# Residual rows of a graph layer: their stores and loads emitted two or three steps later

## The chip, the core and the metric

The kernel runs on one core of a Trainium2 chip. A core has five engines with a queue of instructions each: TensorE (PE) for matrix products, VectorE (DVE), ScalarE (ACT), GpSimd (POOL) and SyncE (SP). They wait for each other only through semaphores. Transfers between the main memory and the core's on-chip memory are issued from the queues of SyncE, ScalarE and GpSimd and carried out by 16 DMA engines. TensorE writes to eight banks of accumulators.

The metric is the device time of one execution in microseconds. A profile shows one execution, instruction by instruction; a time is the median of several executions.

## What is computed

The input `x` holds 8 graphs' features for 4096 nodes and 256 features, `adj` is one matrix of 4096 x 4096, mostly zeros, and `W` is 256 x 256.

```python
HW = jnp.einsum('bnf,fo->bno', x, W)
A_norm = relu((adj + adj.T) * 0.5)
D = jnp.sum(A_norm, axis=1)
d = where(D > 0, D ** -0.5, 0)
L_norm = eye(N) - d[:, None] * A_norm * d[None, :]
out = relu(jnp.einsum('nm,bmo->bno', L_norm, HW))
return layernorm(x + out, axis=-1)      # over the 256 features
```

## The kernel before

**Two stages.** The first symmetrises the matrix block by block, writes it to main memory (`a_dram`), forms the products of features and weights, scaled by the node's degree, and writes them there too (`g_dram`, 4096 rows of 2048 numbers: 8 graphs times 256 features). It also works out, from the pattern of zeros, which rows each block of outputs needs.

The second stage, from about 583 us on, works through the output in 32 blocks of 128 nodes. Block 0 is done in the first stage. The others go in **units** of two blocks, `2u+1` (b0) and `2u+2` (b1), in the order of `SEQ`; the last unit has one block. A unit is a list of **steps**. Each step multiplies gathered rows: a *full* step is four products over the whole array for one block, from a gathered tile or from one of two tiles kept on the chip (hubs); a *row-tiled* step packs up to eight small products of 64 rows x 32 columns, each for four accumulator banks. A gathered tile is 128 rows of `g_dram` (1 MB), fetched by two indirect transfers on GpSimd's queue (lines 956 and 964) into a ring of 12 buffers; a buffer is asked for again once its tile is used up.

**After the products of a block**, `finish` empties its four banks through ScalarE into `y` (line 772, one buffer). VectorE then adds the block's residual row tile `xr` (line 782; 128 nodes x 8 graphs x 256 features, 1 MB), computes mean and variance (line 791) and normalises in place (line 815). SyncE stores the result (line 825). The `xr` tile was loaded before by `residual` (line 766) from ScalarE's queue, into a pool of four buffers which rotates, so that a unit's loads take the buffers of the unit two before it. The last block (31) has its row loaded by GpSimd and is finished by a function of its own.

**What is emitted when.** The program is written out step by step in the loop at line 1209. `after(n, ...)` puts a call on a list; `run_later(2)`, called after each step, lowers each entry by 2 and makes the calls that have 2 or less left. At the start of a unit three calls are put there: `prepare` (6), which gives VectorE the work on the lists of later units, and two of `exchange`. One `exchange` stores the oldest finished block of the unit before (if there is one) and loads the rows that it is given: the first call those of b0, the second those of b1. `finish` itself puts `rest`, the VectorE part of a block, two further on, and `lists` goes there when a unit's b0 is complete: TensorE then counts and places rows for later units (line 430) from what VectorE prepared.

**Order within a queue.** `with queue("act")` and its like pin an instruction behind the last one emitted for that engine. A row-tiled step ends each of its four rounds with a tick, a no-op on ScalarE (line 1206) that waits for TensorE's products of the round; two rounds later TensorE's products wait for it (`follow`). A full step puts nothing into ScalarE's queue. So whatever is emitted for ScalarE after a step stands behind the ticks of the last row-tiled step and behind the last emptying of banks.

**Steps of the units**, in running order, F for full and T for row-tiled, the first seven steps of each: unit 1 and unit 7 FTFFTFT; units 2, 3, 4 and 6 FTFFFTF; unit 5 FTFTFTF; unit 8 FTFTFTT; units 9 to 14 FTFFFTT. Unit 0 and the last unit, 15, load no rows by this path. These units have 11 to 28 steps (unit 15 has 4); b0 ends one or two steps before b1.

Of the kernel before, what the change touches and what calls it, by code (L numbers as in the profile page):

```python
# [67 lines left out]
def kernel(  # L68
# [49 lines left out]
    def blocks(u):  # L118

        return min(2, NB - 1 - 2 * u)  # L120
# [777 lines left out]
    with (  # L898
# [38 lines left out]
        def load_hub_rows(units, h, b):  # L937

            u = next((v for v in units if HUBS[v] > h), None)
            if u is None:  # L940
                return
            i = 2 * u + 1 + b
            with queue("pool"):
                nc.gpsimd.dma_start(
                    hub_rows[h][b], a_dram[h * P : (h + 1) * P, i * P : (i + 1) * P]
                )
            got[u, -1 - h, b] = (hub_rows[h][b], hubs[h], 0, False)
# [26 lines left out]
        def gather_ahead():  # L974
            nonlocal asked, eaten
            while eaten < asked and not uses_left[order[eaten]]:
                eaten += 1
            while asked < len(order) and asked - eaten < RING:
                gather(asked)
                asked += 1  # L980
            if asked == len(order) and asked - eaten < RING and NB - 1 not in xr:
                xr[NB - 1] = ring[asked % RING].rearrange("p (b f) -> p b f", b=B)
                with queue("pool"):
                    nc.gpsimd.dma_start(
                        xr[NB - 1], x[:, (NB - 1) * P :, :].rearrange("b p f -> p b f")
                    )
# [4 lines left out]
        def after(n, fn, *args):  # L991
            later.append((n, fn, args))

        def run_later(by):
            ready = [l for l in later if l[0] <= by]
            later[:] = [(n - by, fn, args) for n, fn, args in later if n > by]
            for _, fn, args in ready:
                fn(*args)
# [63 lines left out]
        def finish(i):  # L1062

            if i == NB - 1:
                while later:
                    run_later(1)
                while finished:
                    exchange([])
                finish_last(i)
                return  # L1070
            with queue("act"):
                y = evict(i, py.pop(i), ypool)

            def rest():
                z = xr.pop(i)
                with queue("dve"):
                    mv, var = moments(i, y, z, stat)
                with queue("dve"):
                    rstd = inverse_root(i, var, stat)

                in_turn(normalise, i, z, mv, rstd)
                finished.append((i, z))

            after(2, rest)
# [80 lines left out]
        def product(u, op, c, ps, cols, start, stop):  # L1165

            t, _, b, _ = op
            at, gt, apart, one = got[u, t] if t >= 0 else got[u, t, b]
            off = -cols.start if one else b * apart
            with queue("pe"):  # L1170
                return nc.tensor.matmul(  # L1171
                    py[2 * u + 1 + b][c][cols, :],
                    lhsT=at[ps, off + cols.start : off + cols.stop],
                    rhs=gt[ps, c * S : (c + 1) * S],
                    start=start,
                    stop=stop,
                    skip_group_check=True,
                )
# [4 lines left out]
        def tiled(u, step, last):  # L1183

            for m in range(NC):
                ins = None
                for i in range(2):
                    c = (m + 2 * i) % NC
                    for op in step:
                        if op[1] != i:  # L1190
                            continue
                        before = ins
                        ins = product(
                            u,
                            op,
                            c,
                            slice(i * L, (i + 1) * L),
                            slice(op[3] * E, (op[3] + 1) * E),
                            False,
                            op in last and m >= NC // 2,  # L1200
                        )
                        if before is None:
                            if len(ticks) > 1:
                                follow(ins, ticks[-2])
                with queue("act"):
                    ticks.append(nc.scalar.nop())
                follow(ticks[-1], ins)

        for q, (u, step) in enumerate(steps):
            new = q == 0 or steps[q - 1][0] != u  # L1210
            if new:
                after(6, prepare, u)
                rows = [2 * u + 1 + b for b in range(2)] if q > 0 and blocks(u) == 2 else []
                if q == 0:
                    after(8, exchange, [])
                elif rows:
                    after(6, exchange, rows[:1])
                    after(10, exchange, rows[1:])
                else:
                    after(2, exchange, [])  # L1220
                    after(4, exchange, [])
                left, begun = {}, set()
                for v, st in steps[q:]:
                    if v == u:
                        for _, _, b, j in st:
                            for e in range(QU) if j is None else [j]:
                                left[b, e] = left.get((b, e), 0) + 1
                for b in range(blocks(u)):
                    py[2 * u + 1 + b] = []
            touched = sorted({b for _, _, b, _ in step})  # L1230
            for b in touched:
                if not py[2 * u + 1 + b]:
                    py[2 * u + 1 + b] = [
                        psum.tile([P, S], F32, tag=f"b{b}", name=f"py_{u}_{b}_{c}") for c in range(NC)
                    ]
            if step[0][1] is None:
                (op,) = step
                b = op[2]
                hs = {(b, e) for e in range(QU)}
                assert not hs & begun or hs <= begun  # L1240
                for h in hs:
                    left[h] -= 1
                for c in range(NC):
                    product(
                        u, op, c, slice(0, P), slice(0, P), not hs & begun, not any(left[h] for h in hs)
                    )
                begun |= hs
            else:
                for op in step:
                    assert op[2:] in begun  # L1250
                    left[op[2:]] -= 1
                last = [op for op in step if not left[op[2:]]]
                tiled(u, step, last)
            for op in step:
                t = op[0]
                uses_left[u, t] -= 1
                if t < 0:
                    load_hub_rows(SEQ[SEQ.index(u) + 1 :], -1 - t, op[2])
            gather_ahead()
            run_later(2)  # L1260
            for b in touched:
                if not any(left[b, e] for e in range(QU)):
                    if b == 0:
                        after(2, lists, u)
                    finish(2 * u + 1 + b)
# [67 lines left out]
```

## Time and profile before

| | us |
|---|---|
| median of 3 timed runs | 1755.12 |
| lowest, highest | 1754.09, 1763.07 |
| the profiled execution's own time | 1499.77 |
| its span, first to last instruction | 1497.7 |
| TensorE busy in it | 1386.5 |
| VectorE busy | 1041.9 |
| GpSimd busy | 766.3 |
| ScalarE busy | 361.2 |
| 28 residual loads from ScalarE, first and last issue | 677.0, 1422.5 |
| 31 stores from SyncE, first and last issue | 595.7, 1474.9 |

The profiled execution took 255 us less than the median of the timed runs; its mean granted clock of TensorE was 0.971. The DMA engines moved 543.04 MB at a mean of 363 GB/s.

In the profile's lines a name such as `xr<-in_x_dram` reads "written from", `L766` is a line of the kernel, and `[5.33 <-...]` is the idle time of the engine ahead of the instruction and what ended it. ACTq and SPq are the queues of ScalarE and SyncE, where transfers are issued. Forty slices of equal length show each engine's busy share in tenths.

### The profile page before, as it was taken

The page shows a single profiled execution, that of the slowest core. Times are in us where ns is not written, and L with a number is a line of the kernel's source. Part 1 is how long each engine was busy: PE and PEld are TensorE (multiplying, and loading weights), DVE is VectorE, ACT ScalarE, POOL GpSimd, SP SyncE. Part 2 cuts the span into 40 slices and gives each one's busy share as a digit, 9 for nine tenths or more (in the row PEclk, how much of TensorE's full clock was granted, in tenths as well). Part 3 has the DMA queues.
Part 4 walks back from the last instruction along what each step waited for, and adds up shares of the span by engine and source line. Part 5 has one row for each costly group of instructions (what it writes and reads, how often), then busy time and mean ns, then how long its engine had stood idle before and what let it go on. Part 6 is the DMA issues. An engine that isn't in the chain of part 4 may idle for free.

```text
span 1497.7 us, 29688 instructions
## 1 busy us (share of the span) xinstructions
PE 1386.5 (93%) x11008; PEld 746.5 (50%) x11008; DVE 1041.9 (70%) x3173; ACT 361.2 (24%) x462; POOL 766.3 (51%) x1564
## 2 busy tenths in 40 slices
PE   7999979999999989999999999999998999898993
PEld 6777857876777753443433333333333333333331
DVE  4677578779594863119477888789229989979554
ACT  4555544554444450010101100100010011011111
POOL 2435010011222326765775777777556776777662
PEclk9999999999999999999999999999999999998996
DMA  9999999998998999999999999999879999999993
GB/s 349 364 377 381 402 402 352 379 379 322 385 370 323 338 381 361 387 390 345 368 384 343 385 401 375 375 391 385 354 262 345 341 373 406 383 351 396 384 378 136
DMA packets 217159, 543.04 MB, mean 363 GB/s; under 512 B 19369, under 2 KB 109193, under 8 KB 182425
## 3 DMA queue, kind: packets, MB, share of 16 engines
q0 software_dynamic: 55664, 283.87, 49.2%
q1 hardware_dynamic: 93472, 126.89, 24.6%
q10 hardware_dynamic: 67872, 130.32, 23.1%
q8 instruction: 89, 1.46, 0.4%
q14 instruction: 62, 0.51, 0.1%
HBM read 438.03 MB, written 136.34 MB: 383 GB/s over the span
## 4 chain that ended last, share of the span: by engine, by line
PE 58%; DMA 21%; DVE 13%; issue 3%; ACT 2%; POOL 2%; ACTq 0%; DVEq 0%; POOLq 0%
PE py L1171 34%; PE pg L606 10%; DMA g<-g_dram,gi 9%; PE lead L564 6%; DMA a_dram<-sym 5%; PE tr L495 3%; PE xtr L595 3%; DVE sym L499 3%; DMA xr<-in_x_dram 3%; DMA xin<-in_x_dram 2%; DVE sums L506 1%; DVE stats L791 1%; DMA ga<-a_dram,ai 1%; DVE xr L782 1%; ACT sym L503 1%
## 5 line engine op out<-in xcount | busy, mean ns | idle before, releaser
L1171 PE MATMUL py<-g,ga 64*32 64x512 f32 (+1 forms) x7136 | 623.3, 610 | 32.0 <-DMA g<-g_dram,gi 28.9
L1171 PEld LDWEIGHTS py<-g,ga 64*32 64x32 f32 (+1 forms) x7136 | 226.3, 114 | 412.6 <-issue 335.9
L956 POOL DMA_INDIRECT ga<-a_dram,ai x268 | 295.4, 1102 | 139.5 <-PE py L1171 67.6
L964 POOL DMA_INDIRECT g<-g_dram,gi x268 | 292.3, 1091 | 117.9 <-issue 71.3
L772 ACT ACTIVATE y<-py,minus_r 128x512 f32<-128x512 f32 x120 | 72.8, 689 | 793.3 <-PE py L1171 551.8
L606 PE MATMUL pg<-w_sb,xt 128*128 128x256 f32 x1024 | 231.2, 384 | 9.3 <-ACT xt L596 9.3
L1171 PE MATMUL py<-g_hub,gh 128*128 128x512 f32 x480 | 220.7, 601 | 5.3 <-DVE pos_k L239 5.3
L606 PEld LDWEIGHTS pg<-w_sb,xt 128*128 128x128 f32 x1024 | 195.2, 193 | 36.7 <-ACT xt L596 10.2
L499 DVE TENSOR_TENSOR sym<-tr,adj 128x512 f32<-128x512 f32 x256 | 162.9, 683 | 66.3 <-PE tr L495 53.8
L506 DVE TENSOR_REDUCE sums<-sym 128x64 f32<-128x2048 f32 x64 | 145.5, 2280 | 58.7 <-ACT sym L503 58.7
L507 POOL TENSOR_SCALAR uses<-sums 128x64 uint8<-128x64 f32 x64 | 24.4, 381 | 268.5 <-DVE sums L506 222.5
L1171 PEld LDWEIGHTS py<-g_hub,gh 128*128 128x128 f32 x480 | 87.6, 190 | 133.0 <-issue 119.7
L495 PE MATMUL tr<-ident,adj 128*128 128x128 f32 x1024 | 136.4, 281 | 17.1 <-DVE sym L499 10.9
L503 ACT ACTIVATE sym<-sym 128x2048 f32<-128x2048 f32 x64 | 122.5, 1915 | 110.4 <-DVE sym L499 104.4
L442 DVE TENSOR_SCALAR low<-lists 128x17 f32<-128x17 f32 (+8 forms) x14 | 2.5, 176 | 202.4 <-PE lists L430 202.4
L495 PEld LDWEIGHTS tr<-ident,adj 128*128 128x128 f32 x1024 | 115.7, 143 | 48.2 <-DVE sym L499 28.7
L782 DVE TENSOR_TENSOR xr<-xr,y 128x2048 f32<-128x2048 f32 x31 | 70.9, 2287 | 51.9 <-ACT y L772 39.3
L595 PE MATMUL xtr<-ident,xin 128*128 128x128 f32 x512 | 73.7, 291 | 19.4 <-DVE sym L499 11.9
L815 DVE TENSOR_SCALAR xr<-xr,mv,root 128x256 f32<-128x256 f32 x248 | 85.2, 416 | 1.1
L791 DVE BATCH_NORM_STATS2 stats<-xr 128x6 f32<-128x256 f32 x248 | 84.1, 412 | 1.1
L564 PE MATMUL lead<-gt,strip 128*128 128x512 f32 x176 | 83.3, 593 | 0.0
L596 ACT COPY xt<-xtr 128x512 f32<-128x512 f32 x128 | 68.1, 592 | 61.3 <-PE xtr L595 59.9
(157 smaller groups left out, 1057.9 us busy)
## 6 DMA issues: line engine op xcount, KB each, us to landing
adj<-in_adj_dram SPq DMA_DIRECT2D x64, 1024.0 KB, 12.2
a_dram<-sym ACTq DMA_DIRECT2D x64, 1024.0 KB, 8.8
out_dram<-xr SPq DMA_DIRECT2D x31, 1024.0 KB, 22.9
xr<-in_x_dram ACTq DMA_DIRECT2D x28, 1024.0 KB, 13.2
xin<-in_x_dram SPq DMA_DIRECT2D x44, 512.0 KB, 11.2
g_dram<-gt ACTq DMA_DIRECT2D x22, 1024.0 KB, 8.0
xin<-in_x_dram POOLq DMA_DIRECT2D x20, 512.0 KB
g_dram<-held ACTq DMA_DIRECT2D x10, 1024.0 KB, 10.2
```

What stands on the lines that cost most here:

```text
L495: ins = nc.tensor.transpose(pt[:, c * P : (c + 1) * P], tji[:, c, a * P : (a + 1) * P], ident)
L499: nc.vector.tensor_add(sym[:, a, :], pt, tij[:, a, :])
L503: nc.scalar.activation(sym, sym, AF.Relu, scale=0.5)
L506: nc.vector.tensor_reduce(sums, sym.rearrange("p a (c q) -> p a c q", q=E), AX.X, ALU.add)
L564: nc.tensor.matmul(lead[c], lhsT=strip, rhs=g[:, c * S : (c + 1) * S], start=not done, stop=len(done) == NB - 1, skip_group_check=True,)
L595: nc.tensor.transpose(pt[:, k, c, :], xin[b // H][:, b % H + k, c * P : (c + 1) * P], ident)
L606: ins = nc.tensor.matmul(pg[:, k * FO : (k + 1) * FO], lhsT=xt[:, b + k, c, :], rhs=w_sb[:, c, :], start=(c == 0), stop=(c == FC - 1),)
L782: nc.vector.tensor_add(z, z, y)
L791: nc.vector.bn_stats(stats[:, b, :], z[:, b, :])
L956: nc.gpsimd.indirect_dma_start(out=at if both else at[:, : E if one else P], out_offset=None, in_=a_pairs if both else a_groups if one els ...
L964: nc.gpsimd.indirect_dma_start(out=gt, out_offset=None, in_=g_dram, in_offset=bass.IndirectOffsetOnAxis(ap=gi[:, t : t + 1], axis=0), boun ...
L1171: return nc.tensor.matmul(py[2 * u + 1 + b][c][cols, :], lhsT=at[ps, off + cols.start : off + cols.stop], rhs=gt[ps, c * S : (c + 1) * S], ...
```

## The change

Two numbers in the loop at line 1209. For units 1 to 14 the two calls of `exchange` are put on the list at 8 and 14 instead of 6 and 10, so that they are made after the steps 3 and 6 of a unit, counted from 0, instead of 2 and 4. The calls for unit 0 and for the last unit stay.

```diff
                 if q == 0:
                     after(8, exchange, [])
                 elif rows:
-                    after(6, exchange, rows[:1])
-                    after(10, exchange, rows[1:])
+                    after(8, exchange, rows[:1])
+                    after(14, exchange, rows[1:])
                 else:
                     after(2, exchange, [])
                     after(4, exchange, [])
```

## The prediction

> **What bounds the kernel now.** I read the page first (slices, waits), then the timelines of ScalarE, SyncE and VectorE around the moved transfers, the waits of TensorE step by step, the DMA share of one unit, and last the chain of waits near the end. Units are counted in running order, 0 to 15, steps within a unit from 0.
>
> ```profile
> span 1497.7 us, 29688 instructions
> ...
> PE   7999979999999989999999999999998999898993
> ...
> DVE  4677578779594863119477888789229989979554
> ...
> DMA  9999999998998999999999999999879999999993
> ```
>
> The changed stage begins at 583 us (slice 16). TensorE is the bound in it, at nearly full share, with the DMA engines full beside it and VectorE near full in slices 30 to 36. So a moved transfer matters only where TensorE waits for data or where VectorE is late. ScalarE's timeline shows where the residual loads (line 766) really go out:
>
> ```profile
> 1131.24 0.37 ACTq L766 DMA_DIRECT2D xr<-in_x_dram  x1
> ...
> 1173.58 1.01 ACTq L766 DMA_DIRECT2D xr<-in_x_dram  x2
> ...
> 1225.98 1.09 ACTq L766 DMA_DIRECT2D xr<-in_x_dram  x2
> ```
>
> In units 9 and 10 (second and third line) both loads of a unit leave 0.4 us apart, though they are emitted two steps apart. A load enters ScalarE's queue behind the last tick (the no-op of line 1206), and only a row-tiled step has ticks; a full step of four products has none. Ten of the fourteen units that load begin full, tiled, full, full, full, so both loads hang on the tick of step 1.
>
> The stores are different. VectorE's and SyncE's timelines:
>
> ```profile
> 1186.75 2.02 DVE L815 TENSOR_SCALAR xr<-xr,mv,root 128x256 f32<-128x256 f32 x6
> ```
> ```profile
> 1188.79 0.37 SPq L825 DMA_DIRECT2D out_dram<-xr  x1
> ```
>
> The normalisation ends at 1188.77 and the store goes at 1188.79. SyncE has nothing else to do, so all 31 stores follow their data within 0.1 us, wherever they are emitted.
>
> TensorE's waits of this stage, here in step 8 of unit 9, and the DMA around it:
>
> ```profile
> 1197.21 1.05 PE L1171 MATMUL py<-g,ga 64*32 64x512 f32 x4 [0.25 <-ACTq L1206]
> 1201.64 4.73 PE L1171 MATMUL py<-g,ga 64*32 64x512 f32 x54 [3.38 <-DMA g<-g_dram,gi]
> ```
> ```profile
> 1180.00:1193.00 13.00, 11.90 (x113) 3.95 (x111) 12.18 (x69) 0.00 (x0) 8.96 (x11) 1.00 1.04 407
> 1193.00:1206.00 13.00, 9.08 (x122) 3.16 (x128) 12.52 (x32) 0.00 (x0) 9.67 (x9) 0.87 1.04 397
> ```
>
> The last three columns are granted clock, DMA share and GB/s: TensorE waits for a gather exactly where the DMA is full, and afterwards runs at a lower clock. A step lasts 3.4 us; this one takes 8.7.
>
> The chain of waits near the end names the other side, a load that is late, and VectorE's timeline shows what its add waited:
>
> ```profile
> 1377.28 0.38 ACTq L766
> 1377.75 45.14 DMA xr<-in_x_dram
> 1423.02 2.30 DVE xr L782
> ```
> ```profile
> 1423.02 2.29 DVE L782 TENSOR_TENSOR xr<-xr,y 128x2048 f32<-128x2048 f32 x1 [5.33 <-DMA xr<-in_x_dram]
> ```
>
> So the second load of unit 13 takes 45 us and is already late. The page's 13.2 us to landing is a median over the few loads it could pair, mostly first ones.
>
> **What the Trainium skill says.** "DMA: Bandwidth & Descriptors", section Queues, rings and completion order: each DMA engine takes turns between the queues that have work, and one queue's descriptors are consumed in ring order. The trace agrees: of the two loads issued at 1173.6 and 1174.0, the packets that close the first have landed by 1185.9 and those of the second by 1205.6. The same page, Issuing engines are not separate DMA queues: loads, stores and gathers share the 16 engines, as the 1.04 share shows. "TensorE: Matmul & The Clock Gate", HAM oscillation: a wait of some microseconds on data drops the clock to half for a while; the clock records here have half-clock windows of 3.4 to 6.8 us at 942, 997, 1201 and 1297, each at a wait for a gather.
>
> **The change, part by part.** Nothing is added or removed. The list is drained by 2 after each step: a due value of 6 fires after step 2, 10 after step 4, 8 after step 3, 14 after step 6.
>
> 1. Stores: emitted later, issued when the data is there; the normalisations end before or near the new place and SyncE has no other work. Cost 0.
>
> 2. First loads: from behind the last tick up to step 2 to the last tick up to step 3. This differs only where step 3 is tiled, in units 5 and 8: from 912.9 to 920.1 and from 1124.1 to 1131.2. Elsewhere 0.
>
> 3. Second loads, the real change. From the last tick up to step 4 to the last one up to step 6. Taking the end of that step in the trace of before plus 1.1 us (tick), unit by unit, issue before, issue after, and landing of the first load of the pair (from the ScalarE queue's packets):
> unit 1: 687.8, 694.8, 682.6; unit 2: 742.5, 756, 748.3; unit 3: 805.6, 819, 812.3; unit 4: 859.6, 873, 879.0; unit 5: 920.1, 927.3, 931.5; unit 6: 969.4, 983, 984.8; unit 7: 1031.8, 1038.9, 1039.5; unit 8: 1131.2, 1141.8, 1129.4; unit 9: 1174.0, 1193.2, 1185.9; unit 10: 1226.4, 1243.4, 1249.8; unit 11: 1273.9, 1293.1, 1288.8; unit 12: 1328.7, 1345.6, 1343.7; unit 13: 1377.8, 1394.7, 1398.4; unit 14: 1422.5, 1434.1, 1437.3.
> So the second load is issued up to 19 us later, but where the first is still in flight then (units 4, 5, 6, 7, 10, 13, 14) it stood in line behind it anyway, and moves nothing. It really starts later by 7 to 13 us in units 1, 2, 3 and 8, 7.3 in 9, 4.3 in 11, 1.9 in 12.
>
> Lateness: before, the second load landed ahead of its add by 40 to 52 us (units 1 to 3), 33 (8), 24.4 (9), 9.4 (10), 20.1 (11), 7.1 (12), 0.7 (13), 0.6 (14). All real shifts fit. Cost 0; if cover is gone, see the second rival.
>
> Gathers: in unit 9 the queue of the loads moves 0.37 MB in 1186 to 1193, which is put behind the gathers that step 8 waits for. At 400 GB/s that is 0.9 us. Unit 11 likewise, 4.3 us at about 60 GB/s, 0.26 MB, 0.6 us. Unit 8: by its wait near 1150 both loads were through; after, about 0.3 MB of the second is not, 0.8 us. Unit 5: the first load starts 7 us later, 0.3 MB, 0.8 us. Sum -3.1 us. Bounds: no more than a whole load, 1.05 MB, can be put behind a wait, 2.6 us in each of units 5 to 11, so -18; and on the other side, early in units 8 and 9 the DMA has spare room (share 0.65 at 1120 to 1125, 0.78 at 1170 to 1175) that the later load no longer uses and asks back where it is full, at most those same two loads, +5.
>
> ScalarE's queue: the issue now stands between the ticks of steps 6 and 7. It takes 0.37 us (0.99 at most) and a semaphore wait of 0.02 before it, and TensorE asks for a tick only two product groups, 0.8 us each, later. 0. The wait for a free buffer held unit 14's second load from 1416.7 to 1422.5 before; its new time is past that. No gain, nothing was waiting there. POOL's queue is untouched; it holds no moved instruction.
>
> Sum: 1497.7 + 2.1 around the span = 1499.8 for the profiled execution, less 3.1, 1496.7. The median of the timed runs is 1755.1, 255 us above; the profile does not say why. I carry the sum over by the ratio 1.17: -3.6 us, 1751.
>
> **Rivals.**
> A. The gathers are freed more than the bytes say. The waits for gathers lengthen steps by 5.6 us in unit 5, 8.2 in 9, 8.8 in 11, 22.6 together, partly by the half-clock windows, which vanish whole if a wait falls below what starts one. If two thirds go, -15, stretched -17: 1738. For it: those windows follow every long wait. Against it: seven units keep their transfers as they were.
>
> B. The second load does not gain from standing in line: the DMA engines are full, and its 20 to 45 us begin with its issue. Then landing moves by the whole shift. Unit 10: 17.0 against 9.4 of slack, 7.6 late; VectorE is full there and unit 11's first step already waits for it (2.6 us), so 7.6 pass on. Unit 12: 9.8, lost in VectorE's idle 1395 to 1406. Unit 14: 11 late, add at 1475, its 11 us of VectorE work ends at 1486 and the last block's VectorE part, begun at 1480.4, waits 5.5. Sum +13, stretched +15: 1770. It decides once a second load of unit 10 lands over 9 us later than before. For it: units 13 and 14 have no slack. Against it: ring order as seen.
>
> C. Nothing that can be told, the forecast's neighbour: moved loads in no critical unit, 1755.
>
> **How the numbers follow.** Forecast with C 0.52, its own range 1744 to 1761; A 0.30; B 0.18. Half a per cent, 8.8 us, is about what a measurement of this kernel tells from no change: the three runs of before already span 9. Faster by more: 0.28 from A and 0.05 of the forecast, 0.33. Slower: 0.16 from B and 0.04, 0.20. Within: 0.47. The range reaches to A and B: 1731 to 1772.
>
> **What would show it.** Stores still at the end of their normalisation; first loads moved only in units 5 and 8; second loads behind a tick of step 5 or 6, alone, with 15 to 30 us to landing in place of 31 to 45; the waits of VectorE for a load in units 13 and 14 as before within 3 us; TensorE's wait in step 8 of unit 9 shorter by about 1 us. It is wrong if second loads of units 10, 13 or 14 land over 5 us later, or if the waits for gathers shrink by more than 10 us in all.

## The result, and the profile after

| | before | after |
|---|---|---|
| median of 22 runs each, us | 1749.35 | 1745.82 |
| lowest, highest | 1737.20, 1763.07 | 1735.45, 1761.93 |
| ratio after / before, 95% interval | | 0.9982 [0.9959, 1.0005] |
| the profiled execution's own time | 1499.77 | 1738.75 |

The change makes no difference that these runs can tell: the interval takes in 1, and all of it lies within half a per cent of 1. Ratios, here and below, leave out runs more than 1.5% slower than the fastest of their kernel, so they can differ a little from the quotient of the medians.

The two profiles cannot be laid side by side, and this has to be cleared first. The page of the kernel after, by slices (busy tenths), has the time of its own runs; the profile of before shown above has not:

```profile
span 1736.6 us, 29690 instructions
...
PE   8999889999998968879887777877895877797774
...
DVE  5675797878765400819193755946045747877346
...
DMA  9999999999999996868786969779559689779983
```

The experiments below show that the same program runs at about 1500 us in some sets of runs and at about 1750 in others, the kernel before and the changed one alike. One set of runs of the changed kernel, the third below, is at 1500. Its page, same view:

```profile
span 1498.6 us, 29690 instructions
...
PE   7999978999999988999999999999899999998983
...
DVE  4667578879595863129477888889119888999544
...
DMA  9999999999999999999999999999878999999994
```

This is the page to hold against the profile of before: a span of 1498.6 beside 1497.7, the DMA engines full in nearly every slice, TensorE nearly full. In the page of 1736.6 the first 15 slices are as busy as before, and then TensorE and the DMA engines both have gaps.

What the edit did to the queues is plain at both levels. ScalarE's timeline (start, length in us, count) for units 9 and 10, first the kernel after, then the changed kernel at 1500 us:

```profile
1362.96 29.40 ACTq L766 DMA_DIRECT2D xr<-in_x_dram  x2
...
1430.73 23.41 ACTq L766 DMA_DIRECT2D xr<-in_x_dram  x2
```

```profile
1180.45 18.00 ACTq L766 DMA_DIRECT2D xr<-in_x_dram  x2
1229.15 17.93 ACTq L766 DMA_DIRECT2D xr<-in_x_dram  x2
```

Each line holds the two loads of a unit; the length runs from the first issue to the end of the second. Before, these two pairs had 1.01 and 1.09 us; now the second load leaves 18 us after the first at 1500 us, and 23 to 29 us after it in the profile of after. So the change does what it says, and it moves the transfer that the prediction said it moves.

### The profile page after: what moved, and what is told of

Read it like the earlier page. It is cut to its first block, busy times and chain, and to the rows that moved or that the text cites. A ratio compares the mean times of both kernels' runs of the same rounds, so it can differ in the third digit from the quotient of the medians.

```text
span 1736.6 us, 29690 instructions
## 1 busy us (share of the span) xinstructions
PE 1452.7 (84%) x11008; PEld 733.8 (42%) x11008; DVE 1044.3 (60%) x3173; ACT 361.1 (21%) x462; POOL 752.2 (43%) x1564
## 2 busy tenths in 40 slices
DMA packets 217159, 543.04 MB, mean 313 GB/s; under 512 B 19369, under 2 KB 109193, under 8 KB 182425
## 4 chain that ended last, share of the span: by engine, by line
PE 64%; another core or an unknown queue 14%; DVE 8%; DMA 6%; issue 5%; ACT 2%; POOL 1%; ACTq 0%; DVEq 0%; POOLq 0%
PE py L1171 43%; PE pg L606 9%; PE lead L564 5%; DMA a_dram<-sym 5%; PE tr L495 3%; DVE sym L499 3%; PE xtr L595 3%; DVE sums L506 1%; ACT sym L503 1%; PE lists L430 1%; DMA g<-g_dram,gi 0%; ACT xt L596 0%; DMA ga<-a_dram,ai 0%; DVE stats L791 0%
## 5 line engine op out<-in xcount | busy, mean ns | idle before, releaser
L1171 PE MATMUL py<-g,ga 64*32 64x512 f32 (+1 forms) x7136 | 689.4, 663 | 209.2 <-ACTq L1206 168.0
L1171 PEld LDWEIGHTS py<-g,ga 64*32 64x32 f32 (+1 forms) x7136 | 214.2, 119 | 666.9 <-issue 331.4
L956 POOL DMA_INDIRECT ga<-a_dram,ai x268 | 275.6, 1028 | 279.9 <-PE py L1171 209.0
L964 POOL DMA_INDIRECT g<-g_dram,gi x268 | 298.0, 1112 | 174.5 <-PE py L1171 89.4
L606 PEld LDWEIGHTS pg<-w_sb,xt 128*128 128x128 f32 x1024 | 194.3, 192 | 36.3 <-ACT xt L596 10.2
```

Of the source, the lines that this page charges most:

```text
L606: ins = nc.tensor.matmul(pg[:, k * FO : (k + 1) * FO], lhsT=xt[:, b + k, c, :], rhs=w_sb[:, c, :], start=(c == 0), stop=(c == FC - 1),)
L956: nc.gpsimd.indirect_dma_start(out=at if both else at[:, : E if one else P], out_offset=None, in_=a_pairs if both else a_groups if one els ...
L964: nc.gpsimd.indirect_dma_start(out=gt, out_offset=None, in_=g_dram, in_offset=bass.IndirectOffsetOnAxis(ap=gi[:, t : t + 1], axis=0), boun ...
L1171: return nc.tensor.matmul(py[2 * u + 1 + b][c][cols, :], lhsT=at[ps, off + cols.start : off + cols.stop], rhs=gt[ps, c * S : (c + 1) * S], ...
```

## The experiments

The theory to test: no part of the change moves anything that TensorE or VectorE waits for. Against it stand the two rivals of the prediction (gathers freed; late second loads passed on) and a question that the numbers raised, which of the two levels of time belongs to what. All ratios are against the kernel before, run beside it on the same chip; the number of runs stands in brackets. Two chips gave 1500 us; a third gave 1750, both times that it was used. The chips of the first comparison and of the first profile are not on record.

**The kernel before, unchanged.** No edit. This is the yardstick: how far two executions of one program differ.

> The kernel before, unchanged, timed against itself: ratio 1.000, and what its interval spans is what no change looks like. Theory (the profiled execution of before, 1499.8 us against 1737 to 1763 us in 22 timed runs, was a rare one): the new profile has a span of 1730 to 1760 us, a mean granted clock near 0.91, and TensorE waits on the ticks of line 1206 of 150 us and more, as the changed kernel's profile has (168 us). Rival (the change itself brought those waits): the span is near 1500 us again, or the waits of TensorE on line 1206 stay under 20 us.

Measured: 1500.49 us (14), beside 1499.90 (51); ratio 1.0006 [0.9995, 1.0018]. The theory, that the profiled execution of 1500 us had been a rare one among runs of 1750, is refuted: here all 65 runs are between 1492 and 1506. Its rival, that the change brought the longer time, is refuted further down, where the kernel before takes 1747 us beside the changed one and the changed one takes 1502. The waits of TensorE for gathers, added over the whole execution (in all, number, longest), of the first profile of before and then of this one:

```profile
PE py L1171 <- DMA g<-g_dram,gi: 28.9, 16, 3.4
```

```profile
PE py L1171 <- DMA g<-g_dram,gi: 31.1, 17, 3.1
```

The total that the prediction meant to lower by 3.1 us differs by 2.2 us between two executions of the same program, and by 6.9 with the next experiment, whose instructions stand in the same order on every engine.

**Stores alone.** The loads stay where they were, the stores go to the new places.

```diff
-        def exchange(rows):
+        def exchange(rows, send=True):
...
-            if finished:
+            if finished and send:
...
-                    after(6, exchange, rows[:1])
-                    after(10, exchange, rows[1:])
+                    after(6, exchange, rows[:1], False); after(8, exchange, [])
+                    after(10, exchange, rows[1:], False); after(14, exchange, [])
```

> The stores are emitted after steps 3 and 6, the loads stay after steps 2 and 4. Theory: a store goes out when its normalisation ends, wherever it is emitted, so every store starts within 0.1 us of the end of its normalisation and the ratio is 1.000 within 0.4%. Rival (the stores' later place is what counts): stores start some us after their data are ready, and the time moves by more than 0.5%.

Measured: 1499.97 us (12); ratio 1.0005 [0.9991, 1.0020]. VectorE's and SyncE's timelines of this kernel, at the store whose place in the profile of before was shown above:

```profile
1191.03 2.67 DVE L815 TENSOR_SCALAR xr<-xr,mv,root 128x256 f32<-128x256 f32 x8
```

```profile
1193.73 0.37 SPq L825 DMA_DIRECT2D out_dram<-xr  x1
```

The normalisation ends at 1193.70 and the store goes at 1193.73. No store of this kernel, of the kernel before or of the changed one begins more than 0.03 us after its data. Moving the emission of the stores moves nothing, because SyncE's queue holds only them and each waits for VectorE. The waits of TensorE for gathers in this execution:

```profile
PE py L1171 <- DMA g<-g_dram,gi: 24.2, 15, 3.1
```

**The loads earlier than before.** The same two numbers, the other way; the stores are emitted earlier with them.

```diff
-                    after(6, exchange, rows[:1])
-                    after(10, exchange, rows[1:])
+                    after(2, exchange, rows[:1])
+                    after(4, exchange, rows[1:])
```

> Both loads earlier than before: first after step 0, second after step 1. Theory: the first loads stand behind the emptying of the banks instead of the tick of step 1, so some 4 us earlier, the second ones still behind the tick of step 1; within 0.4% of before. Rival A (loads in the way of the gathers at a unit's start cost time): slower than before by 5 us or more, as the mirror of a gain by moving them later. Rival B (lateness costs): faster by 5 us or more.

Measured: 1499.07 us (14); ratio 0.9998 [0.9980, 1.0015]. No difference can be told. TensorE's waits for gathers are 21.8 us in all, the least of the profiles at 1500 us: loads put earlier, the opposite of the change, did not lengthen them in this execution.

**The second loads later still.** Three steps further than the change.

```diff
-                    after(6, exchange, rows[:1])
-                    after(10, exchange, rows[1:])
+                    after(8, exchange, rows[:1])
+                    after(20, exchange, rows[1:])
```

> First loads after step 3, second loads after step 9 instead of 6: another three steps, some 10 to 15 us, later. Theory (a second load has room until its add, and the bytes that it takes from gathers are worth under 1 us a unit): 0 to +8 us, the wait of VectorE for xr under 15 us in all. Rival B (lateness of the second load passes to the end): +15 to +30 us, with VectorE waiting 5 us and more for xr in each of units 9 to 14. Rival A (later loads free the gathers): faster than before by 10 us or more.

Measured: 1504.10 us (22); ratio 1.0026 [1.0016, 1.0037], 4 us slower. If later loads freed the gathers, this should have been the larger gain; it is a small loss. TensorE's waits for gathers are 24.5 us in all, inside the 24.2 to 31.1 of the unchanged order.

The wait in step 8 of unit 9, from which the prediction worked out its largest gain, can be read here without the load: the second load of this unit leaves only at 1210.7 us, after the wait. TensorE's timeline and then the window of this kernel (granted clock, DMA share and GB/s at its end):

```profile
1201.62 4.92 PE L1171 MATMUL py<-g,ga 64*32 64x512 f32 x54 [2.16 <-DMA g<-g_dram,gi]
```

```profile
1193.00:1206.00 13.00, 10.84 (x167) 5.11 (x152) 12.42 (x52) 0.00 (x0) 9.96 (x10) 0.88 1.02 374
```

TensorE still waits 2.16 us, beside 3.38 and 2.58 in the two profiles of the kernel before, and the DMA engines are as full without that load: other transfers have taken its place.

Where some of the loss lies is seen on VectorE near the end (start, length, idle time ahead in brackets), of this kernel:

```profile
1470.09 2.29 DVE L782 TENSOR_TENSOR xr<-xr,y 128x2048 f32<-128x2048 f32 x1 [9.77 <-issue]
...
1478.33 4.62 DVE L815 TENSOR_SCALAR xr<-xr,mv,root 128x256 f32<-128x256 f32 x8
1482.87 0.68 DVE L1031 TENSOR_TENSOR g<-g,y 128x512 f32<-128x512 f32 x1
```

and of the kernel before, run again:

```profile
1463.12 2.27 DVE L782 TENSOR_TENSOR xr<-xr,y 128x2048 f32<-128x2048 f32 x1
...
1471.84 2.67 DVE L815 TENSOR_SCALAR xr<-xr,mv,root 128x256 f32<-128x256 f32 x8
1484.69 1.29 DVE L1031 TENSOR_TENSOR g<-g,y 128x512 f32<-128x512 f32 x1 [10.18 <-ACT y L1021]
```

Before, VectorE has idled for 10.2 us when the last block comes (line 1031): unit 14's normalisation is long done. With the load after step 9 the add of unit 14 has itself idled 9.8 us and begins 0.6 us after its load has landed (1469.5 us), its normalisation ends at 1482.9, and the last block queues right behind it without a gap. The stretch from the last weight load to the end of the span is 22.4 us in place of 19.7: 2.7 of the 4 us. The mechanism of the slower rival is real, but it starts beyond the dose of the change. The other 1.5 us or so were not located.

**The change again, three times.** No further edit. The first two sets came at 1750 us, the third at 1500.

> The change itself, beside the kernel before on the same chip, where before takes about 1500 us. Theory: the stage from 583 us on keeps its length within 3 us; ratio 0.998 to 1.001; second loads leave alone, behind the tick of step 5 or 6, and those of units 4, 6, 10, 13 and 14 land within 5 us of where they landed before. Rival A: 10 us or more faster, with TensorE's waits for gathers (24 to 31 us before) under 15. Rival B: 5 us or more slower, with waits of VectorE for xr of more than 10 us together.

Measured: 1745.77 us (14) beside 1747.59 (52); ratio 1.0000 [0.9975, 1.0026].

> The change once more, because the kernel before takes about 1500 us in some calls and about 1750 us in others, and the change has been timed only where it takes 1750. Where before takes 1500: theory, 0 to -3 us, ratio 0.998 to 1.001, second loads of units 4, 6, 10, 13 and 14 landing within 5 us of before although issued 9 to 19 us later; rival B: +5 us or more, as the load after step 9 brought +4. Where before takes 1750: 1.000 within 0.25% again, as second loads land 10 us and more before they are needed there.

Measured: 1746.82 us (14) beside 1749.28 (34); ratio 0.9987 [0.9962, 1.0013].

> The change a third time, for a call in which the kernel before takes about 1500 us. There: 0 to -3 us, ratio 0.998 to 1.001; second loads of units 13 and 14 waited for by 0 to 6 us in all, as before; TensorE's waits for gathers 20 to 31 us as before. Rival B: +3 us or more, all in unit 14's add, as with second loads after step 9. Where before takes 1750: 1.000 within 0.25%.

Measured: 1502.37 us (14) beside 1500.21 (35); ratio 1.0011 [0.9996, 1.0027]. By the ratio that is +1.6 us, from -0.6 to +4.0; the medians differ by 2.2. No difference can be told at either level. When second loads were issued and landed in this execution, read from the ScalarE queue's packets (landing counted from the start of the second stage, which begins between 583 and 587 us):

| unit | latency before, us | latency changed | landing before | landing, unchanged again | landing changed |
|---|---|---|---|---|---|
| 4 | 40.3 | 26.4 | 316.6 | 313.6 | 315.4 |
| 6 | 33.8 | 26.7 | 419.9 | 419.4 | 423.1 |
| 10 | 43.1 | 25.7 | 686.2 | 684.9 | 688.9 |
| 13 | 44.5 | 27.1 | 839.0 | 832.4 | 836.5 |
| 14 | 40.9 | 26.5 | 880.1 | 875.0 | 877.5 |
| 5 | | | 370.0 | 370.4 | 378.9 |
| 8 | | | 561.2 | 557.8 | 587.2 |
| 9 | | | 622.3 | 625.1 | 638.6 |
| 11 | | | 730.3 | 727.8 | 736.5 |
| 12 | | | 786.3 | 772.5 | 786.5 |

The first five rows are loads that had stood in line behind the first of their pair and whose first is still in flight at the new issue: counted from the stage's start they are issued 10 to 20 us later and land within 5 us of where they did. The last five are not covered by a line in this way. In unit 5 the first load leaves later itself, and the second behind it; in unit 8 the first had landed before the second was issued, before the change too; in units 9, 11 and 12 the first has landed when the second leaves, where before it was still in flight. They land 8 to 29 us later than in the unchanged kernel run again, and still ahead of their add (by 5.5 us in unit 12 to 13.2 in unit 11). The add of unit 13, on VectorE's timeline of the changed kernel, which waited 5.33 us before:

```profile
1420.57 2.29 DVE L782 TENSOR_TENSOR xr<-xr,y 128x2048 f32<-128x2048 f32 x1 [4.80 <-DMA xr<-in_x_dram]
```

And the wait in step 8 of unit 9, TensorE's timeline, changed kernel first, then the unchanged one again:

```profile
1204.68 7.90 PE L1171 MATMUL py<-g,ga 64*32 64x512 f32 x107 [2.70 <-DMA g<-g_dram,gi]
```

```profile
1204.09 8.36 PE L1171 MATMUL py<-g,ga 64*32 64x512 f32 x118 [2.58 <-DMA g<-g_dram,gi]
```

2.70 in place of 3.38 looked like the foreseen shortening until the unchanged kernel gave 2.58 at the same place.

**At 1750 us: the second loads after step 11.** On the chip that gave 1750 us.

```diff
-                    after(6, exchange, rows[:1])
-                    after(10, exchange, rows[1:])
+                    after(8, exchange, rows[:1])
+                    after(24, exchange, rows[1:])
```

> First loads after step 3, second loads after step 11, so in units 12 to 14 behind the emptying of b1's banks, and in units 8 to 11 at the end of the unit. Theory (only the lateness in the last unit counts, earlier units lose it again in VectorE's idle time): unit 14's second load is issued at about 1457 and lands 22 us later, its add at about 1480 instead of 1464 to 1470, so +12 to +18 us; rows of units 9 to 13 are waited for by 5 to 20 us each and their waits do not add up. Rival B (every unit's lateness passes on): +35 us or more. Rival (a load needs no lead at all): under +5 us.

Measured: 1747.61 us (22); ratio 1.0008 [0.9988, 1.0028]. At this level five steps more cost nothing that can be told (-2 to +5 us); the +12 to +18 us foreseen were worked out from times of the level at 1500 us, where this kernel was not run. In the profile of after, the first loads land 5 to 11 us after their issue and the second ones 6 to 24, always 9 us or more before their add: nothing about these loads is tight there.

**At 1750 us: 14 MB more.** The kernel before, with a copy of 1 MB from main memory to main memory behind each second load; it adds 14 transfers that the program has no use for.

```diff
-    g_dram = dram.tile([N + 1, G], F32, name="g_dram")
+    g_dram = dram.tile([N + 1, G], F32, name="g_dram"); spare = dram.tile([NB * P, G], F32, name="spare")
...
                     xr[i] = residual(i, nc.scalar)
-
+                    nc.scalar.dma_start(spare[i * P : (i + 1) * P, :].rearrange("p (b f) -> p b f", b=B), x[:, i * P : (i + 1) * P, :].rearrange("b p f -> p b f")) if i % 2 == 0 else None
```

> The kernel before with 14 more transfers of 1 MB, from x to a spare array in main memory, issued from ScalarE behind each second load. They leave the output as it is. Theory (the DMA engines are full in units 4 to 14, so bytes cost their share): 2.6 us each in some 11 units, +20 to +35 us, and the second loads' adds are waited for more. Rival (the DMA engines have room, a queue's turn is what counts): under +8 us, which would also say that bytes put behind the gathers are worth nothing.

Measured: 1755.92 us (13); ratio 1.0049 [1.0018, 1.0080]. Run a second time:

> The 14 more transfers of 1 MB once more. Where before takes 1750 us they cost +8 us, 0.6 us each. Where it takes 1500: theory (the DMA engines are full in most units there), +20 to +35 us, 1.5 to 2.6 us each; rival (room there too): under +10 us.

Measured: 1754.79 us (20); ratio 1.0028 [1.0009, 1.0048]. The queue table of the first of these (packets, MB, share of the 16 engines):

```profile
DMA packets 231720, 557.73 MB, mean 317 GB/s; under 512 B 19593, under 2 KB 123753, under 8 KB 196985
...
q10 hardware_dynamic: 82432, 145.00, 22.4%
```

The copies did run: 557.73 MB where the kernel before moves 543.04. They cost 8.3 and 5.5 us by the medians, 0.4 to 0.6 us per MB, where +20 to +35 us in all were foreseen; a MB in line at 400 GB/s, about the rate in the prediction's windows, would be 2.6. At this level the DMA engines have room, so moving 1 MB by some steps is unlikely to be worth much. It was not tried at 1500 us, where they are full.

**Late only where the end is far.** Second loads after step 9 in the running units up to 12; units 13 and 14 as before.

```diff
-                    after(6, exchange, rows[:1])
-                    after(10, exchange, rows[1:])
+                    after(8 if SEQ.index(u) < 13 else 6, exchange, rows[:1])
+                    after(20 if SEQ.index(u) < 13 else 10, exchange, rows[1:])
```

> As the kernel with second loads after step 9, but units 13 and 14 load after steps 2 and 4 as before. Theory (that kernel's +4 us come from the last two units alone): ratio 1.000 within 0.15%. Rival (they come from the units in the middle, through gathers or VectorE): +3 us or more remain.

Measured: 1749.39 us (14); ratio 1.0020 [0.9992, 1.0047]: this was at 1750 us, where lateness costs nothing anyway, so it tells nothing of the end. At 1500:

> Second loads after step 9 in units 1 to 12 alone, units 13 and 14 as before. Where before takes 1500: theory (the +4 us of second loads after step 9 everywhere arise in the last two units), 1.000 within 0.15%, with unit 14's add waited for as before; rival (they arise in the middle), +3 us or more. Where before takes 1750: within 0.3% of 1.000.

Measured: 1502.46 us (22) beside 1500.21 (35); ratio 1.0015 [1.0000, 1.0029]. The stretch after the last weight load is back at 19.7 us, so that part of the loss did come from the last two units. Whether the whole of it did is not settled: the two intervals, this one and that of all units late, overlap.

## Why the prediction was right

The likeliest case, no difference that can be measured, is what came (1751 us foreseen, 1745.8 measured). By its steps it was right for mixed reasons.

**Stores, 0: shown.** The experiment with the stores alone gives 1.0005, and all stores follow their data within 0.03 us.

**First loads, only in units 5 and 8: shown.** In the changed kernel at 1500 us they leave at 919.5 and 1135.8 us there, four ticks later in ScalarE's queue, behind those of step 3; all others leave behind the same tick as before.

**Second loads stand in line and lose nothing: shown at 1500 us.** The Trainium skill's "DMA: Bandwidth & Descriptors", section Queues, rings and completion order, has one queue's descriptors consumed in ring order, and the first five rows of the table of landings agree: issue 10 to 20 us later, landing within 5 us, latency 26 to 27 us in place of 34 to 45. Unit 5 does not belong here, though the prediction counted it in: its first load leaves later, so its second lands 8.5 us later. This refutes the slower rival for this dose; it would have needed unit 10 to land 9 us later, and unit 10 landed 2.7 us later than in the first profile and 4.0 later than in the second. The later landings of units 5, 8, 9, 11 and 12 stayed inside their slack, as predicted, but some shifts were larger than foreseen: 26 to 29 us in unit 8 and 14 to 16 in unit 9, where the prediction's issue times give 10.6 and it names 7.3. In unit 8 the load left 15 us later, about 4 of them because the units ahead took longer, and it then took 24 us to land in place of 9 to 13; the prediction had moved its start alone. The experiment with step 9 shows where that cover ends, and that the loss then comes out at the place named, the VectorE part of the last block.

**Gathers, -3.1 us: not seen; this term was mis-sized.** At 1500 us the change measures +1.6 us, and -3.1 lies outside the interval of -0.6 to +4.0. The waits for gathers, 26.3 us in all with the change,

```profile
PE py L1171 <- DMA g<-g_dram,gi: 26.3, 13, 3.9
```

are inside the spread of three executions with the same order of instructions, 24.2 to 31.1. Unit by unit, from the first weight load of one to that of the next, in us:

```
unit                5     7      8     9     11    12    14    whole stage
before             56.0  102.9  49.9  52.0  54.9  51.0  40.7  914.4
before, again      56.0  103.5  51.7  48.2  48.6  50.3  47.4  914.8
stores alone       56.1  102.5  51.2  48.5  49.2  50.9  46.5  911.0
change             53.5  110.2  52.2  48.4  48.8  49.7  48.1  915.0
change, step 9     58.4  103.5  52.2  47.8  48.8  49.7  48.5  915.4
```

Units 9 and 11, from whose waits in the first profile half of the term was worked out, are 4 and 6 us shorter in the very next execution of the same program, and the change sits with those. Unit 8, counted at -0.8, has no gain. Only unit 5 is shorter (by 2.5 us where 0.8 was counted), and unit 7 is 7 us longer: there TensorE waits 3.9 us for a gather at 1051 us, while the moved load is in flight (1036 to 1058), a wait that no other of these executions has. The three executions of the old order agree within 1 us in these two units, so both may be the change's doing, a gain in one place and a loss in another; one execution of it does not tell. The step that failed is in the prediction's words "which is put behind the gathers that step 8 waits for": bytes moved out of a window of full DMA were booked as time, when the bytes come back a few microseconds later into engines that are still full, and the wait stays or changes its place. The wait in step 8 of unit 9 shows this most plainly: with the load gone from its window altogether it is still 2.16 us, and the DMA share still 1.02. That the bytes come back as waits elsewhere is the reading which fits the unchanged stage total; no run followed single bytes.

**The faster rival: refuted.** It needed two thirds of 22.6 us of lengthened steps to go. Neither the change nor three steps more takes away anything measurable, and the order of the four doses at 1500 us (steps 0 and 1: 0.9998; before: 1; the change: 1.0011; step 9: 1.0026) leans the other way.

**ScalarE's queue, 0.** No loss can be told from the totals; it was not isolated.

**The carrying over, 1.17: a wrong reason that did no harm.** The prediction scaled its sum from 1499.8 to 1755.1 as if the profiled execution were a lucky one of the same kind. They are two levels with different limits. TensorE's waits, of the kernel after, over the whole execution:

```profile
PE py L1171 <- ACTq L1206: 168.0, 80, 7.5
```

At 1500 us that line is 0.2 us and the waits for gathers lead; at 1750 the waits are put down to ticks, and the queue of loads has room. So nothing allows an effect of full DMA engines at 1500 us to be stretched to 1750, where they are not full. That the first comparison measured -3.5 us, as forecast, is luck and no support for the sum: its interval, -7.2 to +0.9 us, takes in 0, and the two repeats at that level gave -1.8 and -2.5 us with intervals that do as well.

## What to carry to other kernels

Before costing a moved transfer, find what really releases it: here a store follows its data wherever it is emitted, and a load follows the last tick in its queue, so that two of three moves were none. A transfer that stands in line behind another of the same queue can be issued later at no cost, until its slack is used up; look for where that ends (here near the last block, three steps further). Do not book bytes taken out of a full stretch as time won: look first whether the wait is still there when they are gone. And profile the unchanged program twice before pricing a wait of 3 us: units of this one differed by up to 6.7 us from execution to execution with the total the same within half a per cent.

## What the runs showed of the hardware that was not expected

**Two levels of one program.** The kernel before takes 1499.9 and 1500.2 us on two chips and 1747.6 and 1749.3 on a third, and the changed kernel goes with it. Whether it is the chip, or something else that was so while that chip was used, is not settled: it was used twice, within a quarter of an hour. The first stage is the same (581 to 589 us); the second takes 1154 us in the profile of after and 914 at 1500. By long windows (us; busy time and count of TensorE, its weight loads, VectorE, ScalarE and GpSimd; then granted clock, DMA share, GB/s), kernel after and then the changed kernel at 1500 us:

```profile
560.00:1740.00 1180.00, 939.01 (x8168) 327.95 (x8166) 639.27 (x2366) 82.14 (x136) 616.35 (x605) 0.89 0.78 286
```

```profile
560.00:1500.00 940.00, 872.60 (x8171) 342.41 (x8169) 636.90 (x2366) 82.17 (x137) 633.70 (x606) 0.96 0.95 359
```

The work of every engine but TensorE's is the same within 3 per cent, the clock is 0.89 in place of 0.96 and the DMA share 0.78 in place of 0.95. TensorE is busy only 66 us longer, where the spans differ by 238, so most of the difference is waiting. What it waits for stays open. The profile puts 168 us down to ticks, but it holds 10967 records of landings in place of 15123 in the profile of before, most of the missing ones of GpSimd's transfers, and the wait may be on gathers. The chain that ended last points the same way: on each of the seven pages at 1750 us it puts 13 to 17% of the span down to "another core or an unknown queue", in the profile of after 14%, about as much as the difference of 238 us; no page at 1500 us has such a share.

**Waits and the clock.** "TensorE: Matmul & The Clock Gate", section HAM oscillation, has waits on data lower the clock for a while. Here the windows at half clock add up to 279 us in the profile of after and to 90 in that of before. It agrees in direction; how much of the 66 us is the clock was not taken apart.
